# Layer 0 of a graph network: groups of up to eight pairs of slots, one leak and one VectorE sum for each window of 128 nodes

## The chip, the cores and the metric

The kernel runs on one core of a Trainium2 chip. A core has five engines with queues of their own: TensorE (PE, matmuls and transposes), VectorE (DVE), ScalarE (ACT), GpSimd (POOL) and SyncE (SP). Tiles lie in SBUF, 128 partitions wide; TensorE writes to PSUM, which is divided into banks of 512 fp32 values per partition. DMA queues move data between SBUF and the chip's main memory (HBM). The metric is the device time of one execution in microseconds (us), as a median of several runs. Beside it stands one profiled execution with a trace of every instruction; the profiler makes that execution longer.

## The reference

There are 12500 nodes with 64 features and 400000 edges, sorted by target node. Two layers follow each other, each with a residual and a layer norm. Layer 0, which the change touches, computes for every edge a small network of two stages on the target's and the source's features, and sums the results over the edges of each target:

```python
x_i = x[dst]
x_j = x[src]
msg_in = jnp.concatenate([x_i, x_j - x_i], axis=-1)
h = jax.nn.leaky_relu(msg_in @ W1 + b1, NEG_SLOPE)   # slope 0.01
h = jax.nn.leaky_relu(h @ W2 + b2, NEG_SLOPE)
out = jax.ops.segment_sum(h, dst, num_segments=x.shape[0])
...
x = _layernorm(x + _L0_gnn_ref(x, edge_index, ...), axis=-1)
x = _layernorm(x + _L1_gnn_ref(x, edge_index, ...), axis=-1)
```

Layer 1 is an attention over the same edges with four heads: logits from source and target, a softmax over the edges of each target, a weighted sum, a mean over the heads.

## The kernel before, in words

**Windows and slots.** The nodes are ranked by degree and cut into 98 windows of 128. Node p of a window lies on partition p. A window has KW[w] slots, enough for nearly all its nodes' edges; KW falls from 64 in the first window to 19 in the last, 3180 in all. A slot that a node doesn't need points to a row of zeros. What does not fit is handled by separate loops ahead of the layers, which run no rounds on this input.

**Gathers.** Since the first stage is linear, W1's part for the source is computed once per node and put into a table (`btab`, two copies that differ in where a column with the node's rank stands). For every slot, `gather_rows` (L278) lets POOL issue one indirect DMA that fetches the 128 rows of that slot. `fetch0(w)` issues the KW[w] gathers of a window into a buffer `g`, in which two slots stand beside each other as a pair; it first zeroes what the last pair leaves open (L858). Every seven windows it also computes the index lists of the next seven on VectorE (`index_slots`). Layer 1 does the same with its own table, `t1tab` (`fetch1`), whose rows layer 0 writes; it can't start before the last of them is there.

**Groups.** A window's pairs (KW // 2 + 1 of them) are worked on in groups of up to four, 128 x 512 values, one bank of PSUM. `expand` transposes each pair on TensorE (L878), so that the features of two slots lie on the 128 partitions and the nodes along the free dimension; VectorE adds the target's own term (L880), and `leak` applies the leaky relu in place (L884, one scalar_tensor_tensor that reads the tile twice). `second` multiplies by W2, once for each half (L889), and ScalarE adds the bias into a tile `t0` (L891). `leak` runs on that tile too. `collect` multiplies by a matrix that adds the two halves and accumulates over the groups of the window in PSUM (L898); after the last group VectorE sums the four columns of a node (L903). The last pair's second half is copied apart (`ct`, L901): it holds an empty slot, and what the empty slots of a node contributed is taken away again by a multiple of it.

**Per window.** `norm` transposes the sum back (L909), subtracts the empty slots' part (L916, L918), adds the residual, and applies the layer norm (L293 to L300). It also replaces the window's index list by ranks from `g` (L924), after which `g` is free. `logits` prepares layer 1's logits (L931 to L944) and stores two tables over SP (L939, L947).

**Order.** This part is under `tc.manual_schedule()`: each engine executes its instructions in the order in which the program's loop writes them. The loop (L968) is a pipeline by hand over all groups of all windows. In step i it writes `second` of group i-2, then, if a window begins, `fetch0` of the window after next, `expand` and `leak` of group i, `leak` of group i-2's output, and `collect` of group i-4; `norm` and `logits` of a window come one and two steps after its last `collect`, at the end of the step. The groups of a window run from the last pairs to the first. `g` has five buffers, `ht` and `t0` four each, `pt0`, `py0` and `acc0` two banks each.

Of the kernel before, what the change touches and what calls it, by code (L numbers as in the profile page):

```python
# [21 lines left out]
P = 128  # L22
# [40 lines left out]
def tile_gnn_resnorm(ctx: ExitStack, tc: tile.TileContext, x, src, dst, w1, b1, w2, b2,  # L63
# [637 lines left out]
    with tc.tile_pool(name="l0", bufs=1) as l0:  # L701
# [132 lines left out]
        with tc.tile_pool(name="m0", bufs=2) as mp, \  # L834
                tc.tile_pool(name="m0_t", bufs=4) as tp, \
                tc.tile_pool(name="m0_h", bufs=4) as hp, \
                tc.tile_pool(name="m0_x", bufs=3) as xp, \
                tc.tile_pool(name="m0_g", bufs=5) as gp, \
                tc.tile_pool(name="m0_ps", bufs=2, space=PSUM) as mps, \
                tc.manual_schedule():  # L840
            per = G // 2
# [30 lines left out]
            def expand(q):  # L872

                g = bufs[q.w][1]
                n, p0 = q.n, q.p0
                q.pt = mps.tile([P, per, P], F32, name="pt0")
                for p in range(p0, p0 + n):
                    nc.tensor.transpose(q.pt[:, p - p0, :], g[:, p, 1:1 + 2 * D], ident)  # L878
                q.h = hp.tile([P, per, P], F32, name="ht")
                nc.vector.tensor_tensor(q.h[:, :n, :], q.pt[:, :n, :],  # L880
                                        terms[q.w][:, None, :].to_broadcast([P, n, P]), op=ALU.add)

            def leak(x):
                nc.vector.scalar_tensor_tensor(x, x, 0.01, x, op0=ALU.mult, op1=ALU.max)  # L884

            def second(q):
                n = q.n
                py = mps.tile([P, per, P], F32, name="py0")
                nc.tensor.matmul(py[:, :n, :], w2_2, q.h[:, :n, :], start=True, stop=True)  # L889
                q.t = hp.tile([P, per, P], F32, name="t0")  # L890
                nc.scalar.activation(q.t[:, :n, :], py[:, :n, :], AF.Identity, bias=b2_col)  # L891

            def collect(q):

                if q.first:
                    sums[q.w] = mps.tile([D, per, P], F32, name="acc0")
                    cts[q.w] = mp.tile([P, P], F32, name="ct")
                nc.tensor.matmul(sums[q.w][:, :q.n, :], both, q.t[:, :q.n, :], start=q.first,  # L898
                                 stop=q.last)
                if q.p0 + q.n == KW[q.w] // 2 + 1:  # L900
                    nc.scalar.copy(cts[q.w][D:, :], q.t[D:, q.n - 1, :])  # L901
                if q.last:
                    nc.vector.tensor_reduce(cts[q.w][:D, :],  # L903
                                            sums.pop(q.w).rearrange("d j p -> d p j"), AX.X,
                                            ALU.add)

            def norm(w):
                pz = mps.tile([P, P], F32, name="pz", tag="small")
                nc.tensor.transpose(pz, cts.pop(w), ident)  # L909
                xa, g = bufs.pop(w)  # L910

                npad = mp.tile([P, 1], F32, name="npad")
                nc.vector.tensor_scalar(npad, xa[:, XL + 1:XL + 2], float(KW[w]),
                                        float(-2 * (KW[w] // 2 + 1)), op0=ALU.min, op1=ALU.add)
                cn = mp.tile([P, D], F32, name="cn")
                nc.scalar.mul(cn, pz[:, D:], npad)  # L916
                z = mp.tile([P, D], F32, name="z0")
                nc.vector.tensor_add(z, pz[:, :D], cn)  # L918
                nc.vector.tensor_add(z, z, xa[:, :D])
                t1 = tp.tile([P, D1], F32, name="t1")  # L920
                layer_norm(mp, z, t1[:, :D])

                for j in range(2):
                    nc.vector.tensor_copy(idx_all[:, KOFF[w] + j:KOFF[w + 1]:2],  # L924
                                          g[:, :(KW[w] + 1 - j) // 2, j * (2 * DB - 1)])
                rows[w] = t1
# [22 lines left out]
            bufs, terms, sums, cts, rows, done = {}, {}, {}, {}, {}, set()  # L949
            queue = []  # L950
            for w in range(NW):


                pairs = KW[w] // 2 + 1
                qs = [Group(w, p0, min(per, pairs - p0)) for p0 in range(0, pairs, per)]
                assert qs[0].n == per and (pairs % per == 0 or len(qs) > 2)
                qs = qs[::-1]
                if qs[0].n < per and len(qs) > 2:
                    qs[:2] = qs[1::-1]
                qs[0].first = qs[-1].last = True  # L960
                queue += qs
# [6 lines left out]
            for i in range(len(queue) + 7):  # L968
                if 0 <= i - 2 < len(queue):
                    second(queue[i - 2])  # L970
                if i < len(queue):
# [5 lines left out]
                    leak(q.h[:, :q.n, :])  # L977
                    if q.last and q.w + 1 < NW:
                        own_term(q.w + 1)
                if 0 <= i - 2 < len(queue):  # L980
                    q = queue[i - 2]
                    leak(q.t[:, :q.n, :])
                if 0 <= i - 4 < len(queue):
                    q = queue[i - 4]
                    collect(q)
                    if q.last:
                        late[i + 1] = (norm, q.w)
                        late[i + 2] = (logits, q.w)
                if i in late:
                    late[i][0](late[i][1])  # L990
# [243 lines left out]
```

## Time and profile before

| what | value |
|---|---|
| median of 3 runs | 8654.6 us (8643.75 to 8660.56) |
| profiled execution | 10043.12 us |
| its span, first to last instruction | 10041.4 us |
| layer 0's gathers, in the profiled execution | 354 to 5378 us |
| layer 1's gathers, in the profiled execution | 5422 to 9984 us |
| busy: POOL / VectorE / PE / ScalarE | 67% / 42% / 19% / 9% |
| gathers of layer 0, 3180 | 968 ns each, busy 3077.0 us |
| gathers of layer 1, 3180 | 1060 ns each, busy 3370.1 us |
| leaks in layer 0 (L884), 2 x 453 | busy 295.2 and 290.6 us |

How to read the rows: a row of a group gives line, engine, operation, output and inputs with their shape, and the number of instructions; then busy time in us and the mean in ns, then the idle time of the engine just before these instructions and what ended most of it. A row of the timeline begins with start and length in us. "issue" means that the engine waited for nothing that the profile shows, "remote" that the wait ended with a signal that it can't name. TensorE's rows show when an instruction was started, and an end that is modelled. Idle time on an engine which isn't the bound costs nothing.

### The profile page before, as it was taken

What the parts mean: (1) busy time and instruction counts of PE and PEld (TensorE: products, weight loads), DVE (VectorE), ACT (ScalarE), POOL (GpSimd) and SP (SyncE); (2) the same over time, 40 slices, a digit from 0 to 9 for tenths busy, and PEclk for the clock granted to TensorE, in tenths of its full rate; (3) what the DMA queues carried; (4) which work ended last, traced back from release to release, by engine and by line L of the source; (5) the groups of instructions that cost most, each with busy time, mean ns of one, the idle gap of its engine ahead of it and who ended that gap; (6) DMA issues with size and microseconds to landing.
All of it is one profiled execution on the core that took longest, in us unless ns stands there. A gap on an engine that the chain in (4) does not pass through costs nothing. (4 is left out here: it accounts for less than half of the span.)

```text
span 10041.4 us, 30250 instructions
## 1 busy us (share of the span) xinstructions
PE 1901.5 (19%) x5401; PEld 879.9 (9%) x5402; DVE 4229.1 (42%) x6553; ACT 953.2 (9%) x2254; POOL 6736.3 (67%) x6668
## 2 busy tenths in 40 slices
PE   3322323233233232323322000000000000000000
PEld 2201111011111111111111000000000000000000
DVE  3312223122222132223322756566555656566666
ACT  1100001001001010001101000000000000000011
POOL 3465665665665666666655777777777777777775
PEclk9756666566666666666666555555555555555555
DMA  5211111111111111111112111111111111111111
GB/s 108 63 28 22 28 25 27 29 24 26 25 29 27 30 25 29 28 30 27 31 28 30 30 28 28 28 28 28 28 28 28 28 29 28 29 29 29 30 29 23
DMA packets 313178, 308.32 MB, mean 31 GB/s; under 512 B 164924, under 2 KB 204331, under 8 KB 312347
## 3 DMA queue, kind: packets, MB, share of 16 engines
q0 software_dynamic: 216064, 242.80, 12.7%
q1 hardware_dynamic: 96632, 61.87, 2.5%
q10 hardware_dynamic: 282, 1.63, 0.1%
q14 instruction: 153, 1.25, 0.0%
q8 instruction: 47, 0.77, 0.0%
HBM read 262.66 MB, written 43.18 MB: 30 GB/s over the span
## 5 line engine op out<-in xcount | busy, mean ns | idle before, releaser
L278 POOL DMA_INDIRECT g<-btab,idx_all x3180 | 3077.0, 968 | 1833.9 <-issue 1398.8
L278 POOL DMA_INDIRECT g<-t1tab,idx_all x3180 | 3370.1, 1060 | 1112.9 <-issue 1031.2
L880 DVE TENSOR_TENSOR ht<-pt,at 128x512 f32<-128x512 f32 (+3 forms) x453 | 290.5, 641 | 2849.8 <-remote 2030.4
L1128 DVE TENSOR_REDUCE red<-wx 128x256 f32<-128x4096 f32 (+12 forms) x189 | 1388.7, 7348 | 0.1
L1121 DVE TENSOR_TENSOR wx<-g,wt 128x4096 f32<-128x4096 f32 (+12 forms) x189 | 876.6, 4638 | 169.7 <-issue 128.3
L1150 PE MATMUL pn<-ident,nrm 128*128 128x128 f32 x196 | 67.4, 448 | 4389.5 <-DVE nrm L1146 1766.6
L889 PE MATMUL py<-ht,w 128*128 128x512 f32 (+3 forms) x906 | 666.1, 828 | 1154.3 <-DVE ht L880 481.3
L1084 DVE TENSOR_TENSOR lg<-g,ad 128x128 f32<-128x128 f32 (+22 forms) x98 | 29.2, 298 | 1581.7 <-DMA g<-t1tab,idx_all 1332.7
L898 PE MATMUL acc<-t,both 128*64 128x512 f32 (+3 forms) x906 | 588.8, 739 | 0.0
L891 ACT ACTIVATE t<-py,b_col 128x512 f32<-128x512 f32 (+3 forms) x453 | 293.9, 650 | 2820.1 <-remote 1157.4
L1150 PEld LDWEIGHTS pn<-ident,nrm 128*128 128x128 f32 x196 | 28.3, 203 | 4407.6 <-DVE nrm L1146 1749.2
L878 PE MATMUL pt<-ident,g 128*128 128x128 f32 x1663 | 345.8, 341 | 88.5 <-DMA g<-btab,idx_all 86.5
L878 PEld LDWEIGHTS pt<-ident,g 128*128 128x128 f32 x1663 | 283.9, 183 | 413.0 <-issue 394.0
L889 PEld LDWEIGHTS py<-ht,w 128*128 128x128 f32 x906 | 190.4, 260 | 1445.4 <-issue 1234.4
L1087 ACT ACTIVATE lg_low<-lg 128x128 f32<-128x128 f32 (+22 forms) x98 | 27.4, 279 | 2906.2 <-issue 1572.8
L884 DVE SCALAR_TENSOR_TENSOR ht<-ht 128x512 f32<-128x512 f32 (+3 forms) x453 | 295.2, 652 | 15.5
L884 DVE SCALAR_TENSOR_TENSOR t<-t 128x512 f32<-128x512 f32 (+3 forms) x453 | 290.6, 642 | 0.9 <-ACT t L891 0.9
L278 POOL DMA_INDIRECT rt<-etab,first_i x98 | 94.2, 962 | 153.3 <-SPq L400 43.6
L931 PE MATMUL px<-ident,t 128*64 128x128 f32 x98 | 33.4, 341 | 837.0 <-DVE idx_all L924 292.6
L941 DVE TENSOR_TENSOR st<-t,st 128x4 f32<-128x4 f32 x98 | 16.0, 163 | 411.0 <-issue 281.5
L909 PE MATMUL pz<-ident,ct 128*128 128x128 f32 x98 | 38.8, 396 | 782.2 <-DVE ct L903 694.3
L278 POOL DMA_INDIRECT xab<-xtab,node_i x98 | 94.2, 961 | 122.6 <-issue 120.7
(206 smaller groups left out, 2762.8 us busy)
## 6 DMA issues: line engine op xcount, KB each, us to landing
g<-btab,idx_all POOLq DMA_INDIRECT x3180
g<-t1tab,idx_all POOLq DMA_INDIRECT x3180
state<-st SPq DMA_DIRECT2D x98, 134.0 KB
st<-state SPq DMA_DIRECT2D x98, 134.0 KB
xtab<-rt SPq DMA_DIRECT2D x6, 2016.0 KB
btab<-bt SPq DMA_DIRECT2D x2, 3185.0 KB
t1tab<-t SPq DMA_DIRECT2D x98, 34.0 KB
x<-t1tab SPq DMA_DIRECT2D x98, 32.0 KB
```

The source lines that it names most:

```text
L278: nc.gpsimd.indirect_dma_start(out=o, out_offset=None, in_=table[:, :], in_offset=bass.IndirectOffsetOnAxis(ap=idx, axis=0))
L878: nc.tensor.transpose(q.pt[:, p - p0, :], g[:, p, 1:1 + 2 * D], ident)
L880: nc.vector.tensor_tensor(q.h[:, :n, :], q.pt[:, :n, :], terms[q.w][:, None, :].to_broadcast([P, n, P]), op=ALU.add)
L884: nc.vector.scalar_tensor_tensor(x, x, 0.01, x, op0=ALU.mult, op1=ALU.max)
L889: nc.tensor.matmul(py[:, :n, :], w2_2, q.h[:, :n, :], start=True, stop=True)
L891: nc.scalar.activation(q.t[:, :n, :], py[:, :n, :], AF.Identity, bias=b2_col)
L898: nc.tensor.matmul(sums[q.w][:, :q.n, :], both, q.t[:, :q.n, :], start=q.first, stop=q.last)
L909: nc.tensor.transpose(pz, cts.pop(w), ident)
L931: nc.tensor.transpose(px, t1[:, :D], ident)
L1121: nc.vector.tensor_tensor(f.wx[:, :n], f.g[:, j0:j0 + n, None, :D].to_broadcast([P, n, H, D]), f.wt[:, j0:j0 + n, :, None].to_broadcast([P ...
L1128: nc.vector.tensor_reduce(red.rearrange("p h d -> p (h d)"), f.wx[:, :n].rearrange("p k h d -> p (h d) k"), AX.X, ALU.add)
L1150: nc.tensor.transpose(pn[:, j, :], f.nrm[:, 2 * j:2 * j + 2, :], ident)
```

## The change

A group now has up to eight pairs, 128 x 1024 values, and its PSUM tiles span two banks. A window's pairs are cut into eights; where the rest would be under four, the last two groups share it (17 pairs become 8, 5 and 4). That makes 251 groups in place of 453. `second` issues one matmul per bank, and one activation that writes the group's outputs into a tile `t0` for the whole window. `collect` is called once per window, two steps after its last group: one `leak` over all of the window's pairs (128 x 2176 for 17), and one VectorE reduction over the pairs into a 128 x 128 tile. The matmuls with `both` and the copy of the last pair go. `norm` transposes the summed tile and the last pair, and adds the two halves by VectorE after the transposes. `norm` and `logits` of a window stand at the beginning of a step, one and two steps after `collect`. `g` has four buffers, `ht` three, the window tile two, `py0` one of two banks. The last window's groups run from the first pairs to the last. The order of POOL's instructions is the same.

```diff
-            per = G // 2
+            BANK = 512 // P
+            per = 2 * BANK
...
-                q.pt = mps.tile([P, per, P], F32, name="pt0")
+                pt = mps.tile([P, per, P], F32, name="pt0")
...
+                leak(q.h[:, :n, :])
...
             def second(q):
-                n = q.n
-                py = mps.tile([P, per, P], F32, name="py0")
-                nc.tensor.matmul(py[:, :n, :], w2_2, q.h[:, :n, :], start=True, stop=True)
-                q.t = hp.tile([P, per, P], F32, name="t0")
-                nc.scalar.activation(q.t[:, :n, :], py[:, :n, :], AF.Identity, bias=b2_col)
-
-            def collect(q):
-
+                n, p0 = q.n, q.p0
                 if q.first:
-                    sums[q.w] = mps.tile([D, per, P], F32, name="acc0")
-                    cts[q.w] = mp.tile([P, P], F32, name="ct")
-                nc.tensor.matmul(sums[q.w][:, :q.n, :], both, q.t[:, :q.n, :], start=q.first,
-                                 stop=q.last)
-                if q.p0 + q.n == KW[q.w] // 2 + 1:
-                    nc.scalar.copy(cts[q.w][D:, :], q.t[D:, q.n - 1, :])
-                if q.last:
-                    nc.vector.tensor_reduce(cts[q.w][:D, :],
-                                            sums.pop(q.w).rearrange("d j p -> d p j"), AX.X,
-                                            ALU.add)
+                    outs[q.w] = yp.tile([P, KMAX // 2 + 1, P], F32, name="t0")
+                py = pyp.tile([P, per, P], F32, name="py0")
+                for p in range(0, n, BANK):
+                    m = min(BANK, n - p)
+                    nc.tensor.matmul(py[:, p:p + m, :], w2_2, q.h[:, p:p + m, :], start=True,
+                                     stop=True)
+                nc.scalar.activation(outs[q.w][:, p0:p0 + n, :], py[:, :n, :], AF.Identity,
+                                     bias=b2_col)
+
+            def collect(w):
+
+                n = KW[w] // 2 + 1
+                t = outs[w]
+                leak(t[:, :n, :])
+                sums[w] = mp.tile([P, P], F32, name="ts")
+                nc.vector.tensor_reduce(sums[w], t[:, :n, :].rearrange("d j p -> d p j"), AX.X,
+                                        ALU.add)
 
             def norm(w):
-                pz = mps.tile([P, P], F32, name="pz", tag="small")
-                nc.tensor.transpose(pz, cts.pop(w), ident)
+                pz = mps.tile([P, 2, P], F32, name="pz", tag="small")
+                nc.tensor.transpose(pz[:, 0, :], sums.pop(w), ident)
+                nc.tensor.transpose(pz[:, 1, :], outs.pop(w)[:, KW[w] // 2, :], ident)
...
-                cn = mp.tile([P, D], F32, name="cn")
-                nc.scalar.mul(cn, pz[:, D:], npad)
                 z = mp.tile([P, D], F32, name="z0")
-                nc.vector.tensor_add(z, pz[:, :D], cn)
-                nc.vector.tensor_add(z, z, xa[:, :D])
+                nc.vector.scalar_tensor_tensor(z, pz[:, 1, D:], npad, xa[:, :D], op0=ALU.mult,
+                                               op1=ALU.add)
+                nc.vector.tensor_add(z, pz[:, 0, :D], z)
+                nc.vector.tensor_add(z, pz[:, 0, D:], z)
...
-            for i in range(len(queue) + 7):
+            for i in range(len(queue) + 5):
+                for f, w in late.pop(i, ()):
+                    f(w)
                 if 0 <= i - 2 < len(queue):
                     second(queue[i - 2])
...
                     expand(q)
-                    leak(q.h[:, :q.n, :])
...
                     q = queue[i - 2]
-                    leak(q.t[:, :q.n, :])
-                if 0 <= i - 4 < len(queue):
-                    q = queue[i - 4]
-                    collect(q)
                     if q.last:
-                        late[i + 1] = (norm, q.w)
-                        late[i + 2] = (logits, q.w)
-                if i in late:
-                    late[i][0](late[i][1])
+                        collect(q.w)
+                        late.setdefault(i + 1, []).append((norm, q.w))
+                        late.setdefault(i + 2, []).append((logits, q.w))
```

More of the change, by code (lines that the diff above doesn't have):

```diff
@@ L835, in tile_gnn_resnorm @@
                 tc.tile_pool(name="m0_t", bufs=4) as tp, \
-                tc.tile_pool(name="m0_h", bufs=4) as hp, \
+                tc.tile_pool(name="m0_h", bufs=3) as hp, \
+                tc.tile_pool(name="m0_y", bufs=2) as yp, \
                 tc.tile_pool(name="m0_x", bufs=3) as xp, \
-                tc.tile_pool(name="m0_g", bufs=5) as gp, \
+                tc.tile_pool(name="m0_g", bufs=4) as gp, \
                 tc.tile_pool(name="m0_ps", bufs=2, space=PSUM) as mps, \
+                tc.tile_pool(name="m0_py", bufs=1, space=PSUM) as pyp, \
                 tc.manual_schedule():
-            per = G // 2
+            BANK = 512 // P
+            per = 2 * BANK
             raws, own = {}, {}
@@ L875, in expand @@
                 n, p0 = q.n, q.p0
-                q.pt = mps.tile([P, per, P], F32, name="pt0")
+                pt = mps.tile([P, per, P], F32, name="pt0")
                 for p in range(p0, p0 + n):
-                    nc.tensor.transpose(q.pt[:, p - p0, :], g[:, p, 1:1 + 2 * D], ident)
+                    nc.tensor.transpose(pt[:, p - p0, :], g[:, p, 1:1 + 2 * D], ident)
                 q.h = hp.tile([P, per, P], F32, name="ht")
-                nc.vector.tensor_tensor(q.h[:, :n, :], q.pt[:, :n, :],
+                nc.vector.tensor_tensor(q.h[:, :n, :], pt[:, :n, :],
                                         terms[q.w][:, None, :].to_broadcast([P, n, P]), op=ALU.add)
+                leak(q.h[:, :n, :])
             def leak(x):
@@ L947, in logits @@
                 nc.sync.dma_start(state[w * P:(w + 1) * P, :], st)
-            bufs, terms, sums, cts, rows, done = {}, {}, {}, {}, {}, set()
+            bufs, terms, outs, sums, rows, done = {}, {}, {}, {}, {}, set()
             queue = []
             for w in range(NW):
[L954 to L959, printed above, removed]
+                qs, p0, left = [], 0, KW[w] // 2 + 1
+                while left:
+                    n = left if left <= per else per if left >= per + BANK else left - BANK
+                    qs.append(Group(w, p0, n))
+                    p0, left = p0 + n, left - n
+                if w < NW - 1:
+                    qs = qs[::-1]
                 qs[0].first = qs[-1].last = True
```

## The prediction

> **What bounds the kernel now.** I read the engine rows first, then the costliest groups, then the stretches of the two layers.
>
> ```profile
> PE 1901.5 (19%) x5401; PEld 879.9 (9%) x5402; DVE 4229.1 (42%) x6553; ACT 953.2 (9%) x2254; POOL 6736.3 (67%) x6668
> ...
> L278 POOL DMA_INDIRECT g<-btab,idx_all x3180 | 3077.0, 968 | 1833.9 <-issue 1398.8
> L278 POOL DMA_INDIRECT g<-t1tab,idx_all x3180 | 3370.1, 1060 | 1112.9 <-issue 1031.2
> ```
>
> POOL issues 3180 gathers per layer, about 0.95 us each with a regular 0.30 us between two. Nothing else comes near: one gather per slot, one after another on one queue.
>
> ```profile
> 354.00:5378.00 5024.00, 1557.80 (x3887) 637.79 (x3887) 1292.97 (x3459) 468.92 (x1193) 3168.33 (x3275) 0.62 0.14 27
> 5378.00:5422.00 44.00, 26.77 (x77) 10.71 (x77) 25.53 (x86) 13.90 (x44) 0.48 (x1) 0.77 0.08 22
> 5422.00:9984.00 4562.00, 173.32 (x576) 116.92 (x576) 2718.27 (x2592) 380.42 (x773) 3463.99 (x3274) 0.50 0.15 29
> ```
>
> The stretches (columns: span, then busy time of PE, weight loads, VectorE, ScalarE, POOL) are layer 0's gathers, the drain between the layers, layer 1's gathers. In layer 0 POOL is idle 5024.0 - 3168.3 = 1855.7 us; 3275 regular gaps of 0.30 make 983, so about 870 us are real stalls. POOL's waits name them only in part:
>
> ```profile
> POOL g L278 <- issue: 2430.0, 6165, 64.4
> POOL g L278 <- PE px L931: 385.0, 21, 29.6
> ```
>
> They stand before the first gather of a window, where a buffer of `g` or the next batch's indices is late: the compute behind the gathers lags. Why it lags, the timeline shows:
>
> ```profile
> 2797.67 1.06 PE L878 MATMUL pt<-ident,g 128*128 128x128 f32 x4
> ...
> 2816.67 0.69 DVE L880 TENSOR_TENSOR ht<-pt,at 128x512 f32<-128x512 f32 x1 [20.38 <-remote]
> ```
>
> Four transposes start at 2797.67 and take 1.06 us, but the add that waits for them starts at 2816.67. Elsewhere (2832.63 to 2833.26) that step takes 0.6 us. So for long stretches PE's completions reach the others late.
>
> Are these stalls in the timed runs? The profiled execution took 10043.1 us, the median is 8654.6: 1388.5 less. If the 870 us of stalls vanish without the profiler, 518 us remain over 6556 gathers (3180 + 98 per layer): 0.079 us each, a period of 1.25 - 0.079 = 1.17 us. If the stalls stayed and layer 0 kept its length, the 3278 gathers of layer 1 alone would have to give up 0.42 us each, more than the gap of 0.30. I take the first: timed, layer 0 is POOL from end to end, with one gather every 1.17 us, and the compute is hidden behind it (a window has 32.4 gathers on average, 38 us; VectorE is busy 1293/98 = 13 us of it).
>
> **The change, part by part.**
>
> *TensorE.* The 453 sums of pairs (906 matmul records of 0.74 us, 589 us) go; 98 second transposes of 0.40 us come. With 1558 us busy in 5024 PE is not the bound: nothing, hidden under POOL. In the profile, where PE's completions hold the stage back, 3887 records fall to 3079; the profiled span may fall by several hundred us without the median following.
>
> *Groups of eight.* 453 groups become 251. An add or leak of 512 elements takes 0.69 us, of 128 elements 0.29: 0.157 + 1.04 ns per element. Adds fall by 202 x 0.157 = 32 us, the two leaks together from 585 to 498 us, ScalarE's activations by about 50 us; `norm` loses two ScalarE instructions of 0.3 us and gains one of VectorE of 0.23 per window. All hidden under POOL: nothing. One `py` buffer in place of two puts a matmul behind the previous activation (about 1.1 us for 1024 elements); hidden too, about 250 us if POOL were not the bound.
>
> *The new sum.* 98 reductions over 17 pairs (2176 elements) on average. Nearest rows: the reduction of 64x512 takes 0.68 us (1.33 ns per element), that of 128x4096 in layer 1 takes 6.99 us (1.71 ns): 2.9 to 3.7 us each, against 0.68 before, some 220 to 300 us of VectorE. Its 13 us of 38 become 15: hidden.
>
> *Order and buffers.* `norm` and `logits` now stand ahead of the group's own work. Queued behind them are PE's matmuls, VectorE's add and the zeroing of `g`; the chain through PE and ScalarE costs 1 to 2 us per window, and POOL meanwhile has a whole window queued. SP's two stores move with `logits`; nothing else in layer 0 is on SP. Five `g` buffers become four: a gather of window w now needs w-4 in place of w-5 released; `norm` of w-4 does that about one window after its gathers landed, some two windows (76 us) before POOL gets to w. POOL's own instructions keep number and order. The drain between the layers keeps a similar chain (one sum of ten pairs for matmul, copy and reduction): 0, give or take 3 us.
>
> *The leak in one piece.* This is the part on POOL's path. VectorE's leak reads two operands from SBUF, and a gather that starts under it is held:
>
> ```profile
> 2830.64 0.68 DVE L884 SCALAR_TENSOR_TENSOR t<-t 128x512 f32<-128x512 f32 x1
> 2830.67 1.47 POOL L278 DMA_INDIRECT g<-btab,idx_all  x1 [0.30 <-issue]
> ...
> 2832.45 0.95 POOL L278 DMA_INDIRECT g<-btab,idx_all  x1 [0.30 <-issue]
> ```
>
> The leak ends at 2831.32, 0.65 after the gather began; the gather takes 1.47 instead of 0.95, so 0.52 longer: the rest of the leak less about 0.15 (I take 0.17, by other pairs). The gap afterwards is 0.30 as ever, so nothing is made up. All 3180 gathers lose 3077 - 3180 x 0.945 = 72 us so. If a gather can start anywhere under a leak of length D, the mean loss is (D - 0.17)^2 / (2 x 1.25): 0.108 us for 0.69. Over 906 leaks (758 of them full) that is 86 us, times the 0.83 of the stage in which POOL isn't stalled, 71: the row agrees.
>
> What does a leak of 17 pairs cost, 0.157 + 2176 x 1.04 ns = 2.42 us? Two answers. By the row's average, 72 us lost per 585 us of leaks, the 498 us after would lose 61: a gain of 11 us. The Trainium skill speaks against that: "SBUF — State Buffer", in "Who interferes with whom", says that an instruction of VectorE with two SBUF inputs contends with GpSimd's reads, that the shared ports are held for the whole instruction, and that tensor_reduce never contends on this chip. Then the loss grows with the square until D passes the period, and is D - 0.17 - 0.585 beyond it. The trace has one long instruction of this kind:
>
> ```profile
> 84.24 2.06 DVE L590 TENSOR_TENSOR lt<-rt,node_f 128x1792 bf16<-128x1792 uint16 x1
> 84.24 0.95 POOL L278 DMA_INDIRECT rt<-etab,first_i  x1 [0.30 <-issue]
> 85.50 1.62 POOL L278 DMA_INDIRECT rt<-etab,first_i  x1 [0.30 <-issue]
> ```
>
> It ends at 86.30, 0.80 after the second gather's start, and that one is 0.67 longer: held to the end of a 2 us instruction. I take the rule. At a period of 1.17: before, 92 us (POOL never stalls here). After, the 251 first leaks (128 of eight pairs at 1.22 us, 24 of seven, 25 of six, 25 of five, 49 of four, by the cutting rule and the slot counts) lose 85. The 98 long ones lose 2.42 - 0.17 - 0.585 = 1.66 each at a random start, 163 us. But each follows a leak of 5 to 8 pairs at once; a gather held by that one goes through at its end and the next starts some 1.0 us later, well under the long one: 2.42 - 1.0 - 0.17 = 1.25 (the likelier case, by length over period 0.7 to 1), else about 2.07. Mean 1.37, 134 us. Sum: 85 + 134 - 92 = +127 us; with independent starts +156; if the starts fall favourably +75, unfavourably +200.
>
> Does the new reduction hold gathers too? Layer 1's say no:
>
> ```profile
> 7011.88 7.83 DVE L1128 TENSOR_REDUCE red<-wx 128x256 f32<-128x4608 f32 x1
> ...
> 7015.74 0.95 POOL L278 DMA_INDIRECT g<-t1tab,idx_all  x1 [0.30 <-issue]
> 7017.00 0.94 POOL L278 DMA_INDIRECT g<-t1tab,idx_all  x1 [0.30 <-issue]
> ```
>
> Gathers pass in 0.95 in its midst. Nothing, and at most 98 x 3.1 = 304 us if it did.
>
> **Sum:** 8654.6 + 127 = 8782 us; with the ends above 8730 to 8855.
>
> **Rivals.**
> - *Faster: TensorE's late completions are real in the timed runs too.* For it: 2030 us of VectorE's waits are for them, and PE loses a fifth of its records. Against it: the account of the 1388 us above. If a third of the stalls (290 us) are in the timed runs and go, 8654.6 - 290 + 127 = 8492. It decides from the point where more than 127 us of stalls are removed.
> - *No change: a long leak holds no more than the average says* (-11 us), or POOL's losses fall into stalls that remain: about 8645 to 8660. Against it: the 2.06 us instruction.
> - *Much slower: the reduction holds the ports as well*: 8782 + 304 = 9086. Against it: layer 1's gathers.
>
> **How the numbers follow.** Likeliest case 0.73, faster rival 0.14, no change 0.09, reduction 0.04. No change means within 0.2% (17 us, about what a measurement of this kernel can tell). Slower by more: 0.73 + 0.04 = 0.77; within: 0.09; faster: 0.14. The likeliest case's own range is 8715 to 8880 (phases of the starts, and the unknown period). Down to 8560 the range takes in no change and the weakest of the faster cases; up to 8890. Outside it lie most of the faster case (0.11), the reduction (0.04) and the ends of the first (0.05).
>
> **What would show it.** Right: in the changed profile, gathers of `btab` of 2 us and more wherever the leak of 128x2176 runs, their mean up from 968 ns to some 1010, gathers under the new reduction at 0.95, and leaks over 2 us. The waits of the `ht` add for PE may shrink, and the profiled span with them. Wrong: gathers under the long leak that are no longer than 1.5 us; or a median that falls with the profiled span, which would mean that the stalls were never the profiler's.

## The result, and the profile after

| | before | after |
|---|---|---|
| median | 8657.6 us (8643.75 to 8663.75, 4 runs) | 8796.65 us (8794.36 to 8800.71, 4 runs) |
| ratio | 1 | 1.0161, 95% interval 1.0148 to 1.0173 |

The change costs 139 us. The page of the changed kernel, engines and costliest groups (columns as before):

```profile
PE 1547.5 (18%) x4593; PEld 872.8 (10%) x4594; DVE 4487.6 (51%) x5892; ACT 840.5 (10%) x1856; POOL 6530.1 (74%) x6668
...
L278 POOL DMA_INDIRECT g<-btab,idx_all x3180 | 3219.3, 1012 | 976.5 <-issue 944.0
L278 POOL DMA_INDIRECT g<-t1tab,idx_all x3180 | 3010.3, 947 | 1001.1 <-issue 925.4
L883 DVE TENSOR_TENSOR ht<-pt,at 128x1024 f32<-128x1024 f32 (+4 forms) x251 | 261.4, 1042 | 2582.1 <-PE pt L881 2582.1
...
L881 PE MATMUL pt<-ident,g 128*128 128x128 f32 x1663 | 451.7, 391 | 2246.1 <-DMA g<-btab,idx_all 2246.1
```

Layer 0's gathers take 1012 ns each, layer 1's, which are as many, 947. The add waits for PE under its name and no longer for "remote", and PE in turn waits for gathers (2246 us on the transposes' row). So the engines behind POOL wait for it, and not it for them.

The profile shown ahead of the prediction can't be laid beside this one. Its execution took 10043 us, and that was not the profiler's doing, as the text above has it: this span is 8792.5 us in an execution of 8794.36, and the kernel before, profiled again, has a span of 8634.6 in one of 8636.34. Executions of about 10050 us came up again in later sets of runs; what they are is the last section's matter. Until then only kernels of the first set are compared in time, where the kernel before takes 8638.6 us.

The stretches of the kernel before in that second profile (layer 0's gathers, the drain, layer 1's gathers; span, then busy time of PE, weight loads, VectorE, ScalarE, POOL):

```profile
297.20:4464.60 4167.40, 1524.30 (x3926) 581.08 (x3926) 1317.60 (x3498) 471.06 (x1213) 3169.67 (x3275) 0.63 0.19 33
4464.60:4488.80 24.20, 15.05 (x39) 5.36 (x38) 12.69 (x49) 7.37 (x24) 0.09 (x2) 0.78 0.10 25
4488.80:8586.70 4097.90, 173.18 (x576) 116.83 (x576) 2712.35 (x2594) 380.17 (x773) 3094.81 (x3273) 0.50 0.19 32
```

The same of the changed kernel:

```profile
296.90:4612.90 4316.00, 1223.05 (x3138) 637.70 (x3138) 1569.20 (x2852) 366.93 (x827) 3317.73 (x3275) 0.58 0.16 32
4612.90:4638.90 26.00, 7.35 (x18) 3.45 (x18) 13.73 (x32) 3.64 (x12) 0.03 (x1) 0.60 0.06 15
4638.90:8744.80 4105.90, 173.31 (x576) 116.91 (x576) 2712.52 (x2595) 380.29 (x773) 3102.43 (x3273) 0.50 0.16 32
```

Layer 0 is longer by 148.6 us, POOL's busy time in it by 148.1; its idle time is 997.7 and 998.3, one gap of 0.305 between every two gathers. So the whole loss is in the length of the gathers. (A gather that a VectorE instruction makes longer is called held.) Part of the loss is not the change's: every gather of the changed kernel's profile is some 2.5 ns longer, in layer 1 too (4105.9 against 4097.9). In each profile layer 1's sum of 3180 gathers serves as what they take when nothing holds them: 3075.9 - 3003.0 = 72.9 us are lost in layer 0 before, 3219.3 - 3010.3 = 209.0 after, 136 us more of the 139 measured.

Where they are lost, the timeline of one window shows:

```profile
2469.13 0.82 DVE L888 SCALAR_TENSOR_TENSOR ht<-ht 128x640 f32<-128x640 f32 x1
2469.78 0.98 POOL L278 DMA_INDIRECT g<-btab,idx_all  x1 [0.30 <-issue]
2469.87 2.42 DVE L888 SCALAR_TENSOR_TENSOR t<-t 128x2176 f32<-128x2176 f32 x1
2471.07 2.03 POOL L278 DMA_INDIRECT g<-btab,idx_all  x1 [0.30 <-issue]
2472.32 3.79 DVE L908 TENSOR_REDUCE ts<-t 128x128 f32<-128x2176 f32 x1
2473.41 0.95 POOL L278 DMA_INDIRECT g<-btab,idx_all  x1 [0.30 <-issue]
2474.66 0.95 POOL L278 DMA_INDIRECT g<-btab,idx_all  x1 [0.30 <-issue]
```

The gather at 2469.78 starts 0.17 before the first leak ends and loses 0.03; it isn't held by the long leak that begins under way. The next starts at 2471.07, 1.22 before the long leak ends at 2472.29, and is 1.08 longer: what is left of the leak, less 0.14. Over all held gathers of the changed kernel's profile that difference is 0.13 us (quartiles 0.127 and 0.131), where the prediction takes 0.17. Two gathers in the midst of the reduction take 0.95.

### The profile page after: what moved, and what is told of

It reads as the page before. It is cut to its first block, busy times and chain, and to the rows that moved or that the text cites. A ratio compares the mean times of both kernels' runs of the same rounds, so it can differ in the third digit from the quotient of the medians.

```text
span 8792.5 us, 27603 instructions
## 1 busy us (share of the span) xinstructions
PE 1547.5 (18%) x4593; PEld 872.8 (10%) x4594; DVE 4487.6 (51%) x5892; ACT 840.5 (10%) x1856; POOL 6530.1 (74%) x6668
## 5 line engine op out<-in xcount | busy, mean ns | idle before, releaser
L278 POOL DMA_INDIRECT g<-btab,idx_all x3180 | 3219.3, 1012 | 976.5 <-issue 944.0
L278 POOL DMA_INDIRECT g<-t1tab,idx_all x3180 | 3010.3, 947 | 1001.1 <-issue 925.4
L883 DVE TENSOR_TENSOR ht<-pt,at 128x1024 f32<-128x1024 f32 (+4 forms) x251 | 261.4, 1042 | 2582.1 <-PE pt L881 2582.1
L881 PE MATMUL pt<-ident,g 128*128 128x128 f32 x1663 | 451.7, 391 | 2246.1 <-DMA g<-btab,idx_all 2246.1
L899 ACT ACTIVATE t<-py,b_col 128x1024 f32<-128x1024 f32 (+4 forms) x251 | 242.9, 968 | 2012.0 <-PE py L897 2007.8
L908 DVE TENSOR_REDUCE ts<-t 128x128 f32<-128x2176 f32 (+13 forms) x98 | 370.9, 3785 | 3.4
L888 DVE SCALAR_TENSOR_TENSOR ht<-ht 128x1024 f32<-128x1024 f32 (+4 forms) x251 | 261.9, 1044 | 8.6
L888 DVE SCALAR_TENSOR_TENSOR t<-t 128x2176 f32<-128x2176 f32 (+13 forms) x98 | 236.7, 2415 | 1.1 <-ACT t L899 1.1
L297 ACT ACTIVATE ln_sd<-ln_mv,eps_t 128x1 f32<-128x1 f32 x196 | 57.7, 295 | 1443.2 <-DVE ln_mv L295 1443.2
L283 POOL DMA_INDIRECT out_dram<-o,node_i x98 | 97.0, 990 | 63.6 <-issue 28.4
```

The source lines that it names most:

```text
L278: nc.gpsimd.indirect_dma_start(out=o, out_offset=None, in_=table[:, :], in_offset=bass.IndirectOffsetOnAxis(ap=idx, axis=0))
L283: nc.gpsimd.indirect_dma_start(out=table[:, :], out_offset=bass.IndirectOffsetOnAxis(ap=idx, axis=0), in_=i, in_offset=None)
L297: nc.scalar.activation(sd, mv[:, 1:2], AF.Sqrt, bias=eps_t, scale=1.0)
L881: nc.tensor.transpose(pt[:, p - p0, :], g[:, p, 1:1 + 2 * D], ident)
L883: nc.vector.tensor_tensor(q.h[:, :n, :], pt[:, :n, :], terms[q.w][:, None, :].to_broadcast([P, n, P]), op=ALU.add)
L899: nc.scalar.activation(outs[q.w][:, p0:p0 + n, :], py[:, :n, :], AF.Identity, bias=b2_col)
```

## The experiments

### First set: what holds the gathers

**The kernel before, profiled once more.** No edit.

> The kernel before, unchanged, profiled a second time. Theory (the 870 us of stalls in its first profile, and the longer layer 1, belong to that one execution and not to the timed runs): a profile that agrees with the timed runs has no stalls over 1 us in layer 0 beyond a handful, layer 1's gathers at 0.945 us instead of 1.060, the add in layer 0 waiting for no late completions, and a span near 8656 us; its period per gather is 0.945 + 0.305 = 1.25 us and not the 1.17 that the prediction inferred; layer 0's gathers lose 75 to 95 us to the leaks. Rival (the stalls are part of the kernel): about 870 us of stalls again, a span of about 10040 us. If the profiled execution is a disturbed one again (10040 us beside a timed 8655), the first theory stands but its period stays unseen.

8639.4 us (10 runs), beside 8638.6; span 8634.6. Layer 0 has no gap over 0.4 us between gathers, layer 1's gathers take 944 ns, and layer 0's period is 0.944 + 0.305 = 1.25 us.

```profile
L278 POOL DMA_INDIRECT g<-btab,idx_all x3180 | 3075.9, 967 | 976.0 <-issue 945.9
L278 POOL DMA_INDIRECT g<-t1tab,idx_all x3180 | 3003.0, 944 | 998.9 <-issue 938.5
```

The 870 us of stalls are not in these runs. Of the 72.9 us lost, I matched each held gather to the VectorE instruction at whose end it was let go: some 19 us belong to the TENSOR_TENSORs that make the index lists (L261 to L265) and 56 to the leaks (gathers that nothing holds scatter by a few ns, hence 75 and not 72.9). The other order shows too: where a gather starts within 0.03 us after a leak, it isn't held, and that leak takes up to 0.75 us in place of 0.69.

**The outputs' leak with one operand from PSUM.**

```diff
-                nc.scalar.activation(outs[q.w][:, p0:p0 + n, :], py[:, :n, :], AF.Identity,
-                                     bias=b2_col)
+                nc.scalar.activation(outs[q.w][:, p0:p0 + n, :], py[:, :n, :], AF.Identity,
+                                     bias=b2_low, scale=0.01)
+                q.py = py
...
-                leak(t[:, :n, :])
...
+                    t = outs[q.w][:, q.p0:q.p0 + q.n, :]
+                    nc.vector.scalar_tensor_tensor(t, q.py[:, :q.n, :], b2_col, t, op0=ALU.add,
+                                                   op1=ALU.max)
```

> The changed kernel with the leak of the outputs done without a second SBUF input: ScalarE writes 0.01 (y + b) to the window tile, and VectorE takes the maximum of that and y + b from PSUM, group by group (251 instructions of at most 1024 elements in place of 98 of 2176); the order of everything else is kept. Theory (a leak with two SBUF inputs holds a gather that starts under it until its end): the 251 new instructions hold nothing, the about 101 to 134 us that the long leaks cost go: 8797 - 101...134 = 8663 to 8696 us, gathers of btab from 1012 ns to about 972. Rival (the 139 us come from elsewhere: order, four buffers, the reduction): within 20 us of 8797.

8646.8 us, ratio 1.0010 (1.0001 to 1.0019). The changed kernel would stand at 8638.6 x 1.0161 = 8778 in this set, so 131 us are gone. From the page:

```profile
L278 POOL DMA_INDIRECT g<-btab,idx_all x3180 | 3086.7, 971 | 976.1 <-issue 951.1
...
L992 DVE SCALAR_TENSOR_TENSOR t<-py,b_col,t 128x1024 f32<-128x1024 f32 (+4 forms) x251 | 274.5, 1094 | 2.7 <-ACT t L899 2.7
```

VectorE spends more on this leak than before (274.5 us against 236.7), and none of the 251 holds a gather: 81 gathers that start under one, with over 0.15 us of it left, pass unhindered. The first leaks, as many and as long but with both inputs in SBUF, lose 68 us in the same profile. What counts is where the second operand lies. All else that the change did is still in this kernel.

**The first leak with one operand from PSUM.**

```diff
-                nc.vector.tensor_tensor(q.h[:, :n, :], pt[:, :n, :],
+                nc.vector.tensor_tensor(pt[:, :n, :], pt[:, :n, :],
                                         terms[q.w][:, None, :].to_broadcast([P, n, P]), op=ALU.add)
-                leak(q.h[:, :n, :])
+                nc.scalar.mul(q.h[:, :n, :], pt[:, :n, :], 0.01)
+                nc.vector.tensor_tensor(q.h[:, :n, :], pt[:, :n, :], q.h[:, :n, :], op=ALU.max)
```

> The changed kernel with the leak of the first stage done without a second SBUF input: VectorE adds the own term in place in PSUM, ScalarE writes 0.01 of it to SBUF, VectorE takes the maximum of the two; the long leaks stay. One more wait of VectorE for ScalarE per group (about 1 us, behind POOL). Theory: the 85 to 92 us that the first leaks cost go, and each long leak, which now follows nothing that aligns the gathers, costs 1.49 instead of about 1.25 us (+24): 8797 - 85 + 24 = 8736, between 8705 and 8745 us. Rival (only the long leaks matter): about 8797, or above it by the longer chain.

8736.7 us, ratio 1.0112 (1.0095 to 1.0129): 41 us less than 8778, where 61 were expected.

```profile
L278 POOL DMA_INDIRECT g<-btab,idx_all x3180 | 3179.3, 1000 | 976.0 <-issue 947.5
...
L886 DVE TENSOR_TENSOR ht<-pt,ht 128x1024 f32<-128x1024 f32 (+4 forms) x251 | 261.5, 1042 | 236.7 <-ACT ht L885 236.7
...
L889 DVE SCALAR_TENSOR_TENSOR t<-t 128x2176 f32<-128x2176 f32 (+13 forms) x98 | 236.4, 2413 | 2.1 <-ACT t L900 2.1
```

The long leaks alone lose 3179.3 - 3002.8 = 176.5 less 19 for the index lists, 158 us: 1.61 us each. That is near 2.41 - 0.13 - 0.625 = 1.66, a random start, for 17 pairs; the expectation had reckoned with 16 (1.49), which is some 12 of the 20 us. In the changed kernel, where a first leak stands before each, they lose less: 115 us, matched gather by gather. And 237 us of waits of VectorE for ScalarE, which the edit adds, don't appear in the time: they lie behind POOL.

**The window's leak in pieces.**

```diff
-                leak(t[:, :n, :])
+                for p in range(0, n, BANK):
+                    leak(t[:, p:min(p + BANK, n), :])
```

> The changed kernel with the window's leak cut into pieces of four pairs (453 instructions of at most 512 elements, one directly behind the other, 0.69 us each) and nothing else changed; the same elements are read in the same place, VectorE works 98 x 3.6 x 0.157 = 55 us more. Theory (held to the end of the instruction, so the length of one counts and not the sum): by drawing gathers at a period of 1.25 us with random phase against such sequences, the loss of layer 0 falls from 218 to 122 us: 8797 - 96 = 8701 us, gathers of btab near 982 ns. Rival (what counts is VectorE's traffic on SBUF, whatever the length of an instruction): no change or slightly more, 8797 to 8805.

8660.5 us, ratio 1.0027 (1.0017 to 1.0037): 117 us less than 8778.

```profile
L278 POOL DMA_INDIRECT g<-btab,idx_all x3180 | 3097.4, 974 | 976.1 <-issue 949.0
...
L888 DVE SCALAR_TENSOR_TENSOR t<-t 128x512 f32<-128x512 f32 (+3 forms) x453 | 266.7, 651 | 0.5 <-ACT t L899 0.5
```

The same elements, read twice from SBUF in the same place, with VectorE busy 30 us longer, and most of the loss is gone. So it is the length of one instruction that costs, not the traffic.

The gain is larger than the 96 us expected, and by luck. The seven pieces of one window, with the gathers under them:

```profile
451.88 4.07 DVE L888 SCALAR_TENSOR_TENSOR t<-t 128x512 f32<-128x512 f32 x7
453.13 0.94 POOL L278 DMA_INDIRECT g<-btab,idx_all  x1 [0.30 <-issue]
454.38 0.94 POOL L278 DMA_INDIRECT g<-btab,idx_all  x1 [0.30 <-issue]
```

Two pieces take 2 x 4.07 / 7 = 1.16 us, nearly the gathers' period of 1.25, so that a gather which meets a boundary between pieces tends to meet one again two pieces later. Of some 170 gathers that start among the pieces, over 150 start in the last 0.1 us of a piece or within 0.05 us after the start of one, and pass. Only 17 are held, for 7 us in all; at random starts it would be 453 x (0.65 - 0.13)^2 / 2.5 = 49 us, an estimate.

The five kernels together, with the loss in layer 0 taken from the two rows of gathers in each page:

| kernel | lost by gathers, us | more than before | time more than before |
|---|---|---|---|
| before | 72.9 | | |
| outputs' leak by PSUM | 3086.7 - 3003.0 = 83.7 | 10.8 | 8.2 |
| leak in pieces | 3097.4 - 3002.9 = 94.5 | 21.6 | 21.9 |
| first leak by PSUM | 3179.3 - 3002.8 = 176.5 | 103.6 | 98.1 |
| changed (own set) | 3219.3 - 3010.3 = 209.0 | 136.1 | 139.1 |

The gathers' length accounts for every time within 6 us.

### Second to fifth set: sets in which the kernel before takes about 10050 us

**Reduction and leak doubled.** One kernel does the reduction twice, the other leaks the outputs a second time after it (all pairs but the last, whose values `norm` still reads):

```diff
+                ts2 = mp.tile([P, P], F32, name="ts2")
+                nc.vector.tensor_reduce(ts2, t[:, :n, :].rearrange("d j p -> d p j"), AX.X,
+                                        ALU.add)
                 sums[w] = mp.tile([P, P], F32, name="ts")
```

```diff
                 nc.vector.tensor_reduce(sums[w], t[:, :n, :].rearrange("d j p -> d p j"), AX.X,
                                         ALU.add)
+                leak(t[:, :n - 1, :])
```

> The changed kernel with the reduction over a window's pairs done twice, the first time into a tile that nobody reads (98 more instructions of 3.79 us, 371 us of VectorE). Theory (a reduction with one SBUF input holds no gather, and VectorE is hidden behind POOL): 8778 us on a chip where the kernel before takes 8638.6, give or take 6. Rival (a reduction holds as a leak does): + 98 x (3.79 - 0.17 - 0.625) = +293, 9071 us.

> The changed kernel with a second leak of a window's outputs, in place, after their reduction, over all pairs but the last, so that the result stays (98 more instructions of 16.2 pairs on average, 2.3 us each, 225 us of VectorE; they follow a reduction and so meet the gathers at a random phase). Theory: + 98 x (2.31 - 0.17 - 0.625) = +149 us: 8927 where the kernel before takes 8638.6. Rival (the loss of the long leaks is bounded by something else, such as their place at a window's end): + 0 to + 30. Against the doubled reduction, which has more of VectorE's time, this tells what holds the gathers: the two inputs or the work.

The kernel before took 10044.8 us in this set. Two reductions: 10048.5, ratio 1.0004 (0.9986 to 1.0022). Two leaks: 9832.9, ratio 0.9785 (0.9755 to 0.9814). The times say nothing on holds, since POOL's idle time in layer 0 is 768 and 431 us above the 998 us of regular gaps in these profiles; the lengths of the gathers do. Two leaks, then two reductions:

```profile
L278 POOL DMA_INDIRECT g<-btab,idx_all x3180 | 3301.4, 1038 | 1407.0 <-issue 1003.3
...
L888 DVE SCALAR_TENSOR_TENSOR t<-t 128x2176 f32<-128x2176 f32 (+13 forms) x196 | 460.9, 2351 | 4.5 <-ACT t L899 1.1
```

```profile
L278 POOL DMA_INDIRECT g<-btab,idx_all x3180 | 3159.6, 994 | 1744.5 <-issue 1370.2
...
L908 DVE TENSOR_REDUCE ts<-t 128x128 f32<-128x2176 f32 (+13 forms) x98 | 370.9, 3785 | 3.4
L911 DVE TENSOR_REDUCE ts<-t 128x128 f32<-128x2176 f32 (+13 forms) x98 | 369.8, 3773 | 0.0
```

With 224 us more of leaks the gathers lose 3301.4 - 3159.6 = 142 us more than with 370 us more of reductions; 149 were expected for a set without stalls. And two reductions on end in the timeline, with gathers at 0.94 under each:

```profile
1608.10 4.43 DVE L908 TENSOR_REDUCE ts<-t 128x128 f32<-128x2560 f32 x1
1609.18 0.94 POOL L278 DMA_INDIRECT g<-btab,idx_all  x1 [0.30 <-issue]
...
1612.45 4.42 DVE L911 TENSOR_REDUCE ts<-t 128x128 f32<-128x2560 f32 x1
1612.92 0.94 POOL L278 DMA_INDIRECT g<-btab,idx_all  x1 [0.30 <-issue]
```

The two-leaks kernel ran once more, in the fourth set:

> The changed kernel with a second leak of a window's outputs, in place, after their reduction, over all pairs but the last, once more, for the same reason. On a chip where the kernel before takes about 8640: theory + 149 us to 8927 (ratio 1.033), gathers of btab longer by 149/3180 = 47 ns than the changed kernel's 1009; rival (the loss of long leaks is bounded by something else) 8778 to 8808. On a chip like those of the second and third sets the time says nothing and the gathers' length alone is read.

9839.1 us beside 10069.2, ratio 0.9763 (0.9746 to 0.9781). More work and less time, twice: neither theory had foreseen it.

**Both leaks by PSUM**, on the changed kernel (the two edits above together) and on the kernel before (the same edits in its four-pair groups):

> The changed kernel with both leaks done with one operand in PSUM (the two earlier edits together). Beside a kernel before of 8638.6 us, as in the first set of runs, the changed kernel would stand at 8638.6 x 1.0161 = 8778. Theory: only the comparisons with two SBUF operands that make the index lists still hold gathers (about 18 us in the changed kernel's profile); the profile's gathers of btab go to 942 + 18/3.18 = 948 ns, layer 0 to 4087 + 18 = 4105 us, and the time to 8577 us, ratio 0.993 to the kernel before (holds there: 80 us). Rival (the added waits of VectorE for ScalarE cost something of their own): between 8577 and 8640.

> The kernel before (groups of four pairs, sum by matmul) with both leaks done with one operand in PSUM, as in the run beside it. Theory: the holds of its 906 leaks (80 us less about 18 for the index lists) go: 8638.6 - 62 = 8577 us, and it ends within 5 us of the changed kernel with the same edit, which says that groups, sums, order and buffers by themselves cost and bring nothing. Rival (the changed kernel's fewer instructions or other sum are worth something of their own): the two differ by more than 10 us.

10045.4 us, ratio 0.9996 (0.9981 to 1.0010), and 10296.1, ratio 1.0253 (1.0227 to 1.0279). They differ by 251 us, but with POOL stalled for 936 and 1162 us that says nothing on what the expectations weighed, and the question whether groups, sums, order and buffers are worth something by themselves is answered by the first set alone. The first ran twice more, in sets of the same kind:

> The changed kernel with both leaks done with one operand in PSUM once more, because the chip of the second set took 10045 us for the kernel before, with POOL stalled 870 to 950 us in layer 0 by late signals, so that holds of 80 us could not be read from the time there (in its profile the gathers of btab fell to 3008 us, 946 each, as expected). On a chip where the kernel before takes about 8640 and layer 0 has no stalls: theory 8577 us, ratio 0.993. Rival (the added waits of VectorE for ScalarE cost something of their own): between 8577 and 8640. On a chip like that of the second set: a ratio within 0.2% of 1, and the time says nothing.

10087.8 us, ratio 1.0017 (1.0006 to 1.0029).

> The changed kernel with both leaks done with one operand in PSUM, a third time, since two chips took some 10050 us for the kernel before and its layer 0 there stands for signals that come late, whatever the holds. On a chip where the kernel before takes about 8640 and layer 0 has no stalls over 1 us: theory 8577 us, ratio 0.993, gathers of btab 946 ns. Rival (the added waits of VectorE for ScalarE cost something of their own): between 8577 and 8640.

10097.1 us, ratio 1.0026 (1.0016 to 1.0036). The page of the last:

```profile
L278 POOL DMA_INDIRECT g<-btab,idx_all x3180 | 3001.8, 944 | 1965.8 <-issue 1593.0
L278 POOL DMA_INDIRECT g<-t1tab,idx_all x3180 | 3369.8, 1060 | 1117.9 <-issue 1034.9
```

Layer 0's gathers are down to 944 ns, so hardly a hold is left, and the time doesn't follow, because POOL stands idle 1965.8 us before them. What this kernel takes in a set like the first, 8577 us by the sum, has not been measured.

**A filler on POOL.** The odd gain of the two-leaks kernel asked for a test of its own. It holds the gathers most, and its stalls are the smallest. In all these profiles layer 1's 3273 gathers take 4561.6 to 4564.9 us, 1.394 each, whatever the kernel. So something may serve one gather in 1.394 us, and a POOL that issues every 1.25 us runs ahead of it until signals and buffers come late. To test that, POOL was to be slowed, and nothing else:

```diff
                 for j in range(k):
                     gather_rows(g[:, j // 2, (j % 2) * DB:(j % 2 + 1) * DB], btab[j % 2],
                                 idx_all[:, KOFF[w] + j:KOFF[w] + j + 1])
+                    nc.gpsimd.memset(pace, 0.0)
```

> The changed kernel with one tiny zeroing of a tile that nobody reads (128x1) behind each gather of layer 0 on POOL's own queue: 3180 instructions of about 0.10 us (the trace has 0.10 to 0.13 for such), with what POOL needs between two of them 0.10 to 0.20 us each, 320 to 640 us more work for POOL in layer 0. In a set where the kernel before takes about 8640 and POOL never stalls: POOL sets the pace of layer 0, so all of it is paid, ratio 1.0161 + 0.037...0.074 = 1.053 to 1.090; if something else set the pace, less. In a set where the kernel before takes about 10050: theory of a backlog (something that serves a gather in 1.394 us, layer 1's period there whatever the kernel, falls behind a POOL that issues every 1.25 us, signals of other engines come late behind it, and buffers come late): POOL now issues every 1.42 to 1.52 us, there is no backlog, the stalls of 780 us go, layer 0 takes 4650 to 4970 us in place of 5019 and the whole 9705 to 10025 us, no more and likely less than the kernel before. Rival there (signals are late for another reason): the stalls stay and the added work comes on top, 10370 to 10690 us.

9668.2 us beside 10067.5 for the kernel before, ratio 0.9607 (0.9578 to 0.9636): even below the range of the backlog theory. But the edit doesn't slow POOL as meant:

```profile
389.29 0.94 POOL L278 DMA_INDIRECT g<-btab,idx_all  x1 [0.19 <-issue]
390.22 0.12 POOL L866 MEMSET pace<- 128x1 f32 x1
390.53 0.95 POOL L278 DMA_INDIRECT g<-btab,idx_all  x1 [0.19 <-issue]
392.03 0.10 POOL L866 MEMSET pace<- 128x1 f32 x1 [0.55 <-remote]
392.28 0.95 POOL L278 DMA_INDIRECT g<-btab,idx_all  x1
394.13 0.10 POOL L866 MEMSET pace<- 128x1 f32 x1 [0.91 <-remote]
```

The filler lies inside the regular gap: 0.12 us of it and 0.19 idle stand where 0.30 idle stood, and the median of the time from one gather's start to the next is still 1.25 us. What is new is a wait. All fillers write the same tile, so each waits for the signal of the one before (for 3155 of 3179 the trace has no other wait), and POOL stops where that signal is late:

```profile
L278 POOL DMA_INDIRECT g<-btab,idx_all x3180 | 3209.0, 1009 | 621.2 <-issue 537.8
L866 POOL MEMSET pace<- 128x1 f32 x3180 | 365.4, 115 | 352.2 <-remote 270.7
```

The stretch of layer 0 in its profile, then in the one with two reductions (the changed kernel itself was not run in such a set):

```profile
342.60:4989.50 4646.90, 1218.72 (x3100) 648.94 (x3101) 1558.57 (x2823) 365.94 (x812) 3655.98 (x6454) 0.57 0.17 30
```

```profile
354.50:5373.50 5019.00, 1046.07 (x3096) 605.56 (x3096) 1894.71 (x2908) 363.23 (x811) 3252.84 (x3275) 0.57 0.16 27
```

Layer 0 is 372 us shorter. POOL's idle time falls from 1766 to 991 us; that this is nearly the 998 us of regular gaps is chance, since 352 us of it are the fillers' waits. In place of 34 long stalls, 768 us together, POOL now stops some 500 times, for 2.3 us at most. One gather takes 4646.9 / 3275 = 1.419 us on average, near 1.394: 1.25 for the regular period, 0.06 for the leaks' holds and 0.11 for these waits. So a POOL that stops as soon as its own signal is late does better than one that goes on. That fits a backlog; that issuing more slowly would do the same was not tested.

## Why the prediction was right, and where not

- **What bounds the kernel.** POOL does, and the stalls were not in the timed runs: right. The reason given was wrong: not the profiler, but the kind of execution. With that the step to a period of 1.17 us falls. The spans of the two profiles of before differ by 1407 us: 57 ahead of layer 0, 857 in layer 0 (5024 - 4167), 20 in the drain, 464 in layer 1 (4562 - 4098) and 9 behind it. In layer 0 the period is 1.25 us in both kinds when POOL isn't stalled or held. The sum hardly feels it: with 1.25 the leaks of before come to 86 us in place of 92, the first leaks after to 80 in place of 85.
- **TensorE, groups, order, buffers, drain at nothing.** Right: POOL's idle time in layer 0 is 997.7 and 998.3 us, the drain 24.2 and 26.0. VectorE's busy time in layer 0 rises from 1318 to 1569 us, ScalarE's falls from 471 to 367, and neither shows.
- **The new sum.** 3.79 us each, a little above the estimate of 2.9 to 3.7; hidden, and gathers pass under it.
- **The leak in one piece.** The mechanism is right in each part: held to the end of the instruction (less 0.13 us, not 0.17), nothing made up in the gap, cost by length and not by elements. The Trainium skill, "SBUF — State Buffer", section "Who interferes with whom", agrees with the runs: two SBUF inputs hold, one does not (251 leaks with a PSUM operand: none), a reduction doesn't. A remark in that section, that a `tensor_tensor` did not stall a DMA in a probe, doesn't carry over to these gathers, which take their indices from SBUF: in the second profile of before, the TENSOR_TENSOR of L263 held 25 of them, for 5.6 us. By the row's average, the other way weighed there, the change would have gained 11 us.
- **The sizes** of the leaks' costs were all too high, and that their errors cancel is luck. Matched gather by gather, the long leaks cost 115 us where 134 were expected. The shortening by the leak ahead is real: 1.17 each, against 1.61 with that leak gone; 72 of 96 follow a held gather and cost 1.10, not 1.25. The first leaks cost 78 us in place of 85, the leaks of before 56 in place of 92: 115 + 78 - 56 = 137 against 127.
- **The worst term** is the 92 us. "The row agrees" is true of the profile that it was read from: there the leaks lose some 67 us of the 72, the index lists 2. What failed is to carry the random start over to runs in which POOL doesn't stall. In the second profile the starts aren't random: 105 of the 453 first leaks begin within 0.125 us after a gather's start, too late to hold it, where chance would give 45 and the first profile has 43. Why is open; that a group's work starts when its last gather has landed, so that its phase to the gathers isn't free, would explain it and is argued, not shown. The index lists, which the prediction leaves out, cost 18 to 19 us in both kernels and drop out of the difference.
- **The rivals.** Faster: there was no stall to remove. No change: the long leak holds 1.17 us, not what the average says. The reduction: excluded by the gathers under it and by the doubled one.
- **What would show it.** The gathers' mean rose to 1012 ns (1010 expected), about half of those under the long leak reach 2 us and more. The profiled span fell by 1249 us while the median rose; it fell because the second profile was of the other kind, not because PE had fewer records.

## What to carry to other kernels

Where POOL issues transfers back to back, a VectorE instruction with two SBUF inputs that meets them at random costs by the square of its own length up to the period and in full beyond it, so merging such instructions to save their fixed cost can lose more than it saves. Cut them short, or give them one operand in PSUM; the work stays and the holds shrink or go. How much pieces gain hangs on how their length meets the gathers' period, which was favourable here. And look first at whether the profile's execution took the time of the timed runs: if not, find what each stretch has too much before costing an edit on it.

## What was not expected of the hardware

The same kernel runs in 8640 or in 10050 us, in sets of runs as a whole. It isn't a matter of which chip: one chip gave 8638.6 us for the kernel before in the first set and 10069 some 26 minutes later. (The first profile, 10043 us, stands beside timed runs of 8654.6; the record doesn't say whether they were one set.) In the long kind layer 1 takes 1.394 us per gather on average instead of 1.25, with gathers of 1060 ns instead of 944, under every kernel, and in layer 0 signals come late and POOL stalls. In the kernels that ran there, layer 0 is the shorter, the more POOL is occupied:

| kernel | POOL busy in layer 0, us | layer 0, us | ratio to before |
|---|---|---|---|
| before, both leaks by PSUM | 3097.0 | 5256.7 | 1.0253 |
| changed, both leaks by PSUM (second set) | 3098.2 | 5032.0 | 0.9996 |
| changed, two reductions | 3252.8 | 5019.0 | 1.0004 |
| changed, two leaks | 3397.6 | 4826.2 | 0.9785 |
| changed, with the filler | 3656.0 | 4646.9 | 0.9607 |

The first two rows differ in more than POOL's work, and in the last the fillers' work lies in gaps that were idle before; what that kernel adds is POOL's stop at each late signal of its own, and it saves 4%. What serves one gather in 1.394 us there, why signals are late, and why in some sets only, stays open. So does the filler's price in a set like the first. The trace suggests next to none, since 0.115 us fit into a gap of 0.305, but that was not measured. No version was measured that is faster than both kernels in both kinds.
